# A stored instruction order in place of a list scheduler: four transformer layers on one Trainium2 core

## The chip, the cores and the metric

The kernel runs on one core of one Trainium2 chip. Five engines work side by side, each with its own queue that it takes in order: TensorE (PE: matmuls, and PEld for its weight loads), VectorE (DVE), ScalarE (ACT), GpSimd (POOL) and SyncE (SP), which here issues every DMA. The metric is device microseconds of one launch; the times shown are medians, and the profile is that of one execution.

## The reference

The input `x` has 2048 rows of 256 numbers (2 batches of 1024). It passes through four layers, each of a cross-attention and a feed-forward part, which makes eight sub-layers. The context has 77 rows per batch.

```python
x = x + tanh(g_xattn[0]) * attn(layernorm(x), ctx)                      # s0: one head of 256
x = x + tanh(g_ffn[0])   * fp4_ffn(layernorm(x), w_gate, w_up, w_down)  # s1: 704 wide, blocks of 16 rounded to fp4
x = x + tanh(g_xattn[1]) * mha(layernorm(x), ctx, Wq, Wk, Wv, We)       # s2: 16 heads of 16
x = x + tanh(g_ffn[1])   * (relu(layernorm(x) @ W1 + b1) @ W2 + b2)     # s3: 1024 wide
x = x + tanh(g_xattn[2]) * gated_mha(layernorm(x), ctx, w_q, w_kv, ...) # s4: 16 heads of 64
x = x + tanh(g_ffn[2])   * (layernorm(x) @ int4(kernel) + bias + lora)  # s5
x = x + tanh(g_xattn[3]) * mha(layernorm(x), ctx, Wq, Wk, Wv, Wo)       # s6: 16 heads of 16
x = x + tanh(g_ffn[3])   * moe(layernorm(x), 16 experts top 8 + shared) # s7
```

## The kernel before

**Tiles and tasks.** The rows are cut into eight chunks of 256 (`NU` chunks of `NT` = 2 tiles of 128 rows). A chunk going through one sub-layer is a task `u{chunk}s{sublayer}`, so `u5s4` is chunk 5 in sub-layer 4; 64 of these, plus tasks that prepare weights (`f0`, `h1`, `h1b0`, `a2`, `moe` and others). The chunks depend on each other nowhere; within a chunk, the sub-layers follow each other. `x` and all prepared weights stay on chip.

**Precision.** Nearly every product is made as three fp16 matmuls (`mm3`: high by high, high by low, low by high). Splitting a tile into its high and low half (`split`: one ACT pass and one DVE or POOL pass) and transposing it stand between one matmul and the next. Transposes go through PE (`pe_T`, with `ident`) or through a DMA transpose on SP's queue (`dma_T`: 132 of them, 64 on the `b` buffers, which carry probabilities and hidden rows, and 68 on the `m` buffers).

**Two passes of the builder.** `Builder` runs `program` twice. In the first pass no instruction is made: `Plan.note` records each call as an `Op`, with its engine, a duration and a latency by the formulas of `cost` and `dma_cost` (constants `XT`, `LAND`), the buffers that it uses, and the earlier calls that it must follow. Then `Plan.solve` decides the order. In the second pass `Builder.finish` (L558 to L564) issues the calls in `plan.order`, and each engine keeps that order. Every instruction is issued at L562, so the profile shows L562 throughout, and groups are told apart by their tiles. There are 11,317 calls: 6,875 for PE, 1,781 for DVE, 1,428 for ACT, 805 for POOL, 428 for SP.

**What sets the order.** `solve` (L228) is a list scheduler. It gives each call a key (the length of the chain of calls behind it, with a term `bias` for its chunk), runs `forward` (L292), an event-driven walk in which each idle engine takes the ready call with the least key, makes new keys with `backward` from the result, does so `ROUNDS` times, and keeps the best. At the end it adds `SHIFT`, a table of offsets, two per task, to the keys, and runs `forward` once more. `hold_back` (L207) adds edges that keep weight preparation from running too far ahead (`AHEAD`, `GATE`).

**Buffers.** Working tiles come from pools (`BUFFERS`, L48): 23 `m`, 4 `h`, 7 `b`, 32 `s`, 14 `q`, 8 PSUM banks `ps`, and five regions `R1` to `R5`. `forward` gives a tile its place when its first call starts in the walk, and frees the place when its last call ends there; `allowed` refuses a place that could lead to a deadlock. On the chip, the first call on a reused place waits for the last call on the tile that had it before.

Of the kernel before, what the change touches and what calls it, by code (L numbers as in the profile page):

```python
# [18 lines left out]
AX = mybir.AxisListType  # L19
# [3 lines left out]
P = 128  # L23
D = 256
S = 77
NU = 8
# [89 lines left out]
class Plan:  # L116
# [4 lines left out]
    def __init__(self):  # L121
        self.nc = bacc.Bacc("TRN2", target_bir_lowering=False, num_devices=1)
        self.ops = []
        self.places = {}
        self.bufs = []
        self.seen = {}
        self.tasks = []
        self.roots = {}
        self.gates = {}


    def task(self, label, *needs):

        at = {t[1]: i for i, t in enumerate(self.tasks)}
        self.tasks.append((len(self.tasks), label, [at[n] for n in needs if n in at]))
        if label[0] == "u":
            self.gates[int(label[3]), int(label[1])] = len(self.ops)
# [32 lines left out]
    def note(self, engine, name, a, k):  # L170
# [28 lines left out]
        if all(self.ops[j].task == 0 for j in op.pred):  # L199
            self.hold_back(i, op)  # L200
# [6 lines left out]
    def hold_back(self, i, op):  # L207


        label = self.tasks[op.task][1]  # L210
        if label == "setup":
            return
        if label[0] == "u":
            if not op.pred:
                op.pred[i - 1] = 0.0
            return
        roots = self.roots.setdefault(op.task, [])
        ahead = AHEAD.get(label, 3)
        if len(roots) >= ahead:
            j = roots[-ahead]  # L220
            j = max(self.ops[j].succ, default=j)
            op.pred[j] = self.ops[j].t
        elif label in GATE:
            op.pred[self.gates[GATE[label]]] = 0.0
        roots.append(i)


    def solve(self):  # L228


        ops = self.ops
        rest = [0.0] * len(ops)
        for i in range(len(ops) - 1, -1, -1):
            rest[i] = max([ops[i].t + ops[i].lat] + [ops[j].pred[i] + rest[j] for j in ops[i].succ])
        key = [bias(self.tasks[op.task][1]) - r for op, r in zip(ops, rest)]
        best = None
        self.ends = []
        for _ in range(ROUNDS):
            plan = self.forward([(k, i) for i, k in enumerate(key)])
            self.ends.append(plan[0])  # L240
            if best is None or plan[0] < best[0]:
                best, best_key = plan, key
            key = self.backward(plan[2])
        if SHIFT:
            best = self.forward([(k + 100.0 * d, i) for i, (k, d) in enumerate(zip(best_key, self.shifts()))])
            self.ends.append(best[0])
        self.end, self.place, self.start = best
        self.order = sorted(range(len(ops)), key=lambda i: (self.start[i], i))

    def shifts(self):  # L250

        n = len(self.tasks)
        first, last = SHIFT[:n], SHIFT[-n:]
        total = [0] * n
        for op in self.ops:
            total[op.task] += 1
        seen = [0] * n
        for op in self.ops:
            t = op.task
            yield first[t] + (last[t] - first[t]) * (seen[t] / (total[t] - 1) if total[t] > 1 else 0.0)  # L260
            seen[t] += 1

    def backward(self, start):


        ops = self.ops
        begin = [0.0] * len(ops)
        at = [op.t + op.lat for op in ops]
        left = [len(op.succ) for op in ops]
        ready = {e: [] for e in ENGINES}  # L270
        idle = dict.fromkeys(ENGINES, 0.0)
        events = [(op.lat, i) for i, op in enumerate(ops) if not op.succ]
        heapq.heapify(events)
        while events:
            now = events[0][0]
            while events and events[0][0] <= now:
                i = heapq.heappop(events)[1]
                if i >= 0:
                    heapq.heappush(ready[ops[i].engine], (-start[i] - ops[i].t, i))
            for e in ENGINES:  # L280
                if ready[e] and idle[e] <= now:
                    i = heapq.heappop(ready[e])[1]
                    begin[i] = idle[e] = now + ops[i].t
                    heapq.heappush(events, (idle[e], -1))
                    for j, p in ops[i].pred.items():
                        left[j] -= 1
                        at[j] = max(at[j], begin[i] + p)
                        if not left[j]:
                            heapq.heappush(events, (max(now, at[j] - ops[j].t), j))
        return [-b for b in begin]  # L290

    def forward(self, key):  # L292
        ops = self.ops
        n = len(ops)
        left = [len(op.pred) for op in ops]
        at = [0.0] * n


        last = {}
        for i, op in enumerate(ops):  # L300
            for b in op.bufs:
                last[b] = i
        uses = [0] * len(self.bufs)
        todo = [0] * len(self.tasks)
        claim = [dict.fromkeys(BUFFERS, 0) for _ in self.tasks]
        live = {}
        shared = {c for c, (_, m) in BUFFERS.items() if m == 1}
        turn = {}
        for i, op in enumerate(ops):
            todo[op.task] += 1  # L310
            for b in sorted(op.bufs):
                uses[b] += 1
                c, task = self.bufs[b]
                turn.setdefault(c if c in shared else (c, task), {})[b] = None
                if c not in shared:
                    now = live.setdefault((task, c), set())
                    now.add(b)
                    claim[task][c] = max(claim[task][c], len(now))
            for b in sorted(op.bufs):
                c, task = self.bufs[b]  # L320
                if last[b] == i and c not in shared:
                    live[task, c].discard(b)
        turn = {c: deque(q) for c, q in turn.items()}
        most = {c: max(t[c] for t in claim) for c in BUFFERS}
        free = {c: deque(range(m)) for c, (_, m) in BUFFERS.items()}
        held = [dict.fromkeys(BUFFERS, 0) for _ in self.tasks]

        def allowed(b):
            c, task = self.bufs[b]
            if turn[c if c in shared else (c, task)][0] != b:  # L330
                return False
            if not free[c]:
                return False
            if c in shared or len(free[c]) > most[c]:
                return True
            have = {d: len(f) for d, f in free.items()}
            have[c] -= 1
            held[task][c] += 1
            ended = set()

            def ends(t):
                if t in ended or not todo[t]:
                    return True
                if not all(ends(u) for u in self.tasks[t][2]):
                    return False
                if any(claim[t][d] - held[t][d] > have[d] for d in claim[t]):
                    return False
                for d, h in held[t].items():
                    have[d] += h
                ended.add(t)  # L350
                return True

            open_ = {t for t in range(len(self.tasks)) if any(held[t].values())}
            while open_:
                now = {t for t in open_ if ends(t)}
                if not now:
                    break
                open_ -= now
            held[task][c] -= 1
            return not open_  # L360

        place = {}
        stuck = []
        ready = {e: [] for e in ENGINES}
        idle = {e: 0.0 for e in ENGINES}
        queue = [0.0] * 16
        held_till = 0.0

        tick, columns, warm = 0, 0.0, False
        start = [None] * n  # L370
        events = [(0.0, 0, i) for i in range(n) if not left[i]]
        heapq.heapify(events)
        now = 0.0
        end = 0.0
        done = 0
        while events:
            now = events[0][0]
            while events and events[0][0] <= now:
                _, kind, i = heapq.heappop(events)
                if kind == 0:  # L380
                    heapq.heappush(ready[ops[i].engine], key[i])
                elif kind == 1:
                    again = False
                    for b in sorted(ops[i].bufs):
                        uses[b] -= 1
# [1228 lines left out]
```

## Time and profile before

| | |
|---|---|
| median of 7 runs | 869.66 us (865.59 to 873.34) |
| profiled execution, its own time | 869.66 us |
| its span, first to last instruction | 867.8 us |
| PE busy | 788.1 us (91%) |
| DVE busy | 682.8 us (79%) |
| POOL busy | 586.8 us (68%) |
| ACT busy | 553.0 us (64%) |
| mean granted PE clock | 0.956 |

The table's busy times are times in which at least one instruction of the engine was under way. A busy PE is not a PE at full pace: where the granted clock is low, the same matmul stays busy longer. The profile also gives the span in 40 slices, waits by the engine that ended them, and the busy time of each engine in any stretch that one asks for.

### The profile page before, as it was taken

How to read it: one execution, taken by the hardware profiler on the slowest of the kernel's cores; microseconds unless marked ns; L12 is line 12 of the kernel's file. 1: busy time of each engine (PE TensorE's matmuls, PEld its weight loads, DVE VectorE, ACT ScalarE, POOL GpSimd, SP SyncE). 2: the span in 40 equal slices, each digit the busy share in tenths (PEclk: the TensorE clock that was granted, in tenths of full speed). 3: DMA queues.
4: the chain of work that ended last, by engine and by line, in shares of the span. 5: the costliest groups of instructions: out<-in, count | busy, mean ns of one | idle time of the engine just before them, and what ended most of it. 6: DMA issues, size and time to landing. Idle time of an engine off the chain costs nothing.

```text
span 867.8 us, 20178 instructions
## 1 busy us (share of the span) xinstructions
PE 788.1 (91%) x6995; PEld 612.5 (71%) x6995; DVE 682.8 (79%) x1797; ACT 553.0 (64%) x1718; POOL 586.8 (68%) x809
## 2 busy tenths in 40 slices
PE   3889688998789999788998889999999999999998
PEld 2665355554576777566876677788888888888887
DVE  5778999998978977777888877869699886566544
ACT  5789673578674688999749888555465443233331
POOL 4455699999868868778979678967376553243332
PEclk9689799977899999899999999999999999999999
DMA  8453555698896659797996869792949455132411
GB/s 265 132 118 98 138 164 117 129 197 201 162 169 127 116 98 201 153 182 129 193 238 149 166 123 179 138 196 77 217 99 205 102 119 153 37 78 65 129 38 37
DMA packets 288175, 122.19 MB, mean 141 GB/s; under 512 B 236731, under 2 KB 276553, under 8 KB 287817
## 3 DMA queue, kind: packets, MB, share of 16 engines
q1 hardware_dynamic: 288073, 120.90, 64.0%
q8 instruction: 55, 0.90, 0.4%
q14 instruction: 47, 0.39, 0.1%
HBM read 53.71 MB, written 12.10 MB: 76 GB/s over the span
## 4 chain that ended last, share of the span: by engine, by line
PE 37%; DMA 8%; DVE 4%; POOL 3%; ACT 3%; issue 1%; SPq 0%; ACTq 0%; POOLq 0%; DVEq 0%
PE w_ps L562 37%; DMA w_b<-w_b 5%; ACT w_m L562 2%; DVE w_m L562 2%; POOL w_m L562 2%; DMA w_m<-w_m 1%; ACT w_b L562 1%; POOL w_b L562 1%; DMA w_m<-cd 1%; DVE w_s L562 1%; DMA w_b<-qd 0%; DVE w_b L562 0%; DMA qd<-w_m 0%; DVE x L562 0%; DVE w_ps L562 0%
## 5 line engine op out<-in xcount | busy, mean ns | idle before, releaser
L562 PE MATMUL w_ps<-w_m,w_R 128*128 128x256 f16 x2208 | 304.5, 274 | 6.1 <-DVE w_m L562 2.5
L562 PE MATMUL w_ps<-w_R,w_m 128*128 128x256 f16 (+4 forms) x1584 | 295.7, 306 | 7.0 <-DMA w_m<-w_m 2.1
L562 POOL TENSOR_TENSOR w_m<-w_m,w_m 128x256 f16<-128x256 f32 (+1 forms) x200 | 173.0, 878 | 141.6 <-ACT w_m L562 130.8
L562 PEld LDWEIGHTS <-w_m 128*128 128x128 f16 (+2 forms) x1936 | 181.5, 100 | 85.2 <-issue 19.0
L562 PEld LDWEIGHTS <-w_R 128*128 128x128 f16 x2208 | 214.4, 98 | 35.1 <-issue 5.8
L562 PE MATMUL w_ps<-w_R,w_b 128*128 128x256 f16 (+5 forms) x2352 | 210.2, 235 | 28.0 <-DMA w_b<-w_b 9.9
L562 ACT ACTIVATE w_m<-w_m 128x512 f16<-128x512 f32 (+7 forms) x230 | 118.9, 536 | 149.8 <-DVE w_m L562 130.4
L562 PEld LDWEIGHTS <-w_b 128*128 128x128 f16 (+2 forms) x2352 | 161.0, 98 | 68.4 <-issue 29.0
L562 ACT ACTIVATE w_m<-w_ps,w_s 128x77 f32<-128x77 f32 x528 | 146.6, 384 | 23.2 <-DVE w_s L562 15.6
L562 ACT ACTIVATE w_m<-w_ps 128x512 f32<-128x512 f32 (+6 forms) x192 | 93.4, 498 | 63.0 <-PE w_ps L562 47.3
L562 DVE SCALAR_TENSOR_TENSOR w_m<-w_ps,w_m 128x512 f32<-128x512 f32 (+3 forms) x160 | 103.5, 656 | 34.4 <-PE w_ps L562 26.9
L562 POOL TENSOR_TENSOR w_b<-w_m,w_b 128x462 f16<-128x462 f32 (+1 forms) x112 | 106.3, 962 | 31.3 <-ACT w_b L562 26.1
L562 DVE SCALAR_TENSOR_TENSOR w_m<-w_m,w_m 128x512 f32<-128x512 f32 (+3 forms) x92 | 76.8, 839 | 20.1 <-DMA w_m<-cd 11.8
L562 ACT ACTIVATE w_b<-w_m 128x462 f16<-128x462 f32 (+1 forms) x144 | 78.3, 583 | 2.3 <-PE w_ps L562 1.5
L562 DVE TENSOR_REDUCE w_ps<-w_ps 128x6 f32<-128x462 f32 (+2 forms) x104 | 56.1, 560 | 17.6 <-PE w_ps L562 16.5
L562 ACT ACTIVATION_READ_ACCUMULATOR w_m<-w_ps,w_s 128x1 f32 x272 | 66.3, 259 | 0.0
L562 POOL TENSOR_TENSOR w_b<-w_m,w_q 128x704 f16<-128x704 f16 (+2 forms) x48 | 53.5, 1132 | 6.2 <-DVE w_m L562 3.6
L562 POOL TENSOR_TENSOR w_s<-w_s,mhalf 128x2 f32<-128x2 f32 (+1 forms) x73 | 55.2, 759 | 3.5 <-DVE w_s L562 0.8
L562 DVE SCALAR_TENSOR_TENSOR x<-w_ps,sg_None,x 128x512 f32<-128x512 f32 (+1 forms) x56 | 37.3, 666 | 21.9 <-PE w_ps L562 21.6
L562 DVE BATCH_NORM_STATS2 w_s<-x 128x6 f32<-128x256 f32 x128 | 49.8, 410 | 6.0 <-DMA x<-in_x_dram 5.6
L562 POOL TENSOR_TENSOR w_m<-w_m,w_s 128x462 f32<-128x462 f32 (+1 forms) x48 | 43.3, 908 | 14.3 <-DVE w_s L562 11.5
L562 POOL TENSOR_TENSOR w_R<-w_m,w_R 128x512 f16<-128x512 f32 (+1 forms) x46 | 47.8, 1047 | 1.6 <-ACT w_R L562 1.1
(139 smaller groups left out, 1015.8 us busy)
## 6 DMA issues: line engine op xcount, KB each, us to landing
w_m<-cd SPq DMA_DIRECT2D x64, 256.0 KB
w_b<-qd SPq DMA_DIRECT2D x32, 256.0 KB
w_m<-in_l_gu_dram SPq DMA_DIRECT2D x17, 256.0 KB
qd<-w_m SPq DMA_DIRECT2D x16, 256.0 KB
w_m<-in_l_w_dram SPq DMA_DIRECT2D x10, 256.0 KB
AD<-w_h SPq DMA_DIRECT2D x8, 308.0 KB
w_R<-AD SPq DMA_DIRECT2D x2, 1232.0 KB
BD<-w_b SPq DMA_DIRECT2D x8, 308.0 KB
```

The source lines that it names most:

```text
L562: r = f(*a, **k)
```

## The change

The list scheduler goes (`forward`, `backward`, `shifts`, `hold_back`, `bias` and their tables). In its place stands `ORDER`, a compressed list of all 11,317 call numbers, found beforehand by a local search over an in-order simulation of the engines. `solve` unpacks it and hands out the buffers along it: a tile gets a place at its first call in the list, and the place goes back to the end of its pool's queue at the tile's last call in the list. The recorded calls themselves, the engine of each and the sizes of the pools stay. Two constants of the DMA cost formula change as well.

```diff
     def note(self, engine, name, a, k):
...
-        if all(self.ops[j].task == 0 for j in op.pred):
-            self.hold_back(i, op)
...
     def solve(self):
-        ops = self.ops
-        rest = [0.0] * len(ops)
-        for i in range(len(ops) - 1, -1, -1):
-            rest[i] = max([ops[i].t + ops[i].lat] + [ops[j].pred[i] + rest[j] for j in ops[i].succ])
-        key = [bias(self.tasks[op.task][1]) - r for op, r in zip(ops, rest)]
...
-        if SHIFT:
-            best = self.forward([(k + 100.0 * d, i) for i, (k, d) in enumerate(zip(best_key, self.shifts()))])
-            self.ends.append(best[0])
-        self.end, self.place, self.start = best
-        self.order = sorted(range(len(ops)), key=lambda i: (self.start[i], i))
+        steps = np.frombuffer(zlib.decompress(base64.b85decode("".join(ORDER))), "<i2")
+        self.order = [int(i) for i in np.cumsum(steps.astype(np.int64))]
+        assert sorted(self.order) == list(range(len(self.ops)))
+        uses = [0] * len(self.bufs)
+        for op in self.ops:
+            for b in op.bufs:
+                uses[b] += 1
+        free = {c: deque(range(m)) for c, (_, m) in BUFFERS.items()}
+        self.place = {}
+        for i in self.order:
+            for b in sorted(self.ops[i].bufs):
+                c = self.bufs[b][0]
+                if b not in self.place:
+                    self.place[b] = free[c].popleft()
+            for b in sorted(self.ops[i].bufs):
+                uses[b] -= 1
+                if not uses[b]:
+                    free[self.bufs[b][0]].append(self.place[b])
...
-XT = 20.0
-LAND = {"T": 1400.0, "R": 1900.0, "W": 500.0}
+XT = 22.0
+LAND = {"T": 1600.0, "R": 2200.0, "W": 600.0}
...
-AHEAD = {"a2": 6, "moe": 6, "f0": 9, "h1": 6, "h3": 6, "f1": 6}
...
-ROUNDS = 6
-
-SHIFT = [
-    -1145, 40, -1870, -735, 359, 42, 673, 54, -910, 81, -384, -5505, -489, -282, 121, 400, 154, 296, -437, -12,
...
-]
-BIAS = [i * 12 for i in range(8)]
...
+ORDER = (
...
+)
```

## The prediction

> **What bounds the kernel now.** I read the page first: busy shares, then the 40 slices, then the waits of PE, and then a table of stretches that I cut by PE's own progress.
>
> ```profile
> PE 788.1 (91%) x6995; PEld 612.5 (71%) x6995; DVE 682.8 (79%) x1797; ACT 553.0 (64%) x1718; POOL 586.8 (68%) x809
> ...
> PE   3889688998789999788998889999999999999998
> ...
> DVE  5778999998978977777888877869699886566544
> ...
> PEclk9689799977899999899999999999999999999999
> ```
>
> PE is the engine to feed, but the slices show two regimes. Up to the eleventh slice (239 us) DVE stands at 7 to 9 while PE has gaps and its granted clock falls; after that PE is nearly full, and over the last fifth it never stops.
>
> ```profile
> PE w_ps L562 <- DVE w_m L562: 12.3, 13, 2.1
> PE w_ps L562 <- DMA ident<-in_c_ident_dram: 12.0, 1, 12.0
> PE w_ps L562 <- DMA w_b<-w_b: 9.9, 10, 2.3
> PE w_ps L562 <- ACT w_m L562: 8.9, 12, 1.7
> PE w_ps L562 <- ACT w_b L562: 6.8, 10, 1.2
> PE w_ps L562 <- DVE w_q L562: 6.6, 3, 6.2
> ```
>
> No single wait is worth a prediction: apart from the start (12.0 us) and one of 6.2 us, they are 1 to 2 us each, ended by every engine and by DMAs. This is what an order can change, and it has to be summed by stretch.
>
> How the stretches were cut: I paired the n-th record of each engine with the n-th call of that engine in the order. For each shape of matmul I took a low (20th percentile) start-to-start time as its full-pace price: 109 ns for the 4,384 of 256 columns, 25 ns for those of 51 and fewer, 194 ns for 462. That makes 717.4 us of PE work, and the cuts lie at each twentieth of it (35.9 us). The last five are one line.
>
> ```profile
> 0.00:75.50 75.50, 55.60 (x333) 39.48 (x333) 53.75 (x203) 56.94 (x155) 37.80 (x59) 0.84 0.59 159
> 75.50:134.90 59.40, 47.09 (x256) 27.58 (x255) 57.07 (x146) 43.42 (x103) 46.78 (x40) 0.89 0.54 145
> 134.90:183.50 48.60, 43.62 (x242) 25.13 (x240) 44.60 (x120) 28.56 (x75) 46.21 (x48) 0.89 0.62 132
> 183.50:239.00 55.50, 47.36 (x374) 29.41 (x373) 51.17 (x131) 40.87 (x125) 48.39 (x64) 0.85 0.87 186
> ...
> 357.60:406.60 49.00, 40.97 (x399) 30.43 (x398) 33.07 (x106) 47.50 (x213) 36.10 (x59) 0.93 0.78 148
> 406.60:446.80 40.20, 37.73 (x414) 30.55 (x413) 34.59 (x87) 24.83 (x65) 33.04 (x65) 1.00 1.08 218
> 446.80:490.10 43.30, 38.89 (x306) 28.46 (x305) 36.82 (x108) 36.09 (x152) 36.97 (x59) 0.96 0.86 185
> ...
> 569.10:607.30 38.20, 36.62 (x360) 32.36 (x359) 29.95 (x60) 19.05 (x40) 28.52 (x42) 1.00 0.58 130
> ...
> 683.00:867.80 184.80, 180.73 (x1731) 159.98 (x1727) 115.95 (x239) 62.61 (x125) 68.61 (x71) 1.00 0.30 82
> ```
>
> Columns: stretch, length, busy time of PE, PEld, DVE, ACT, POOL, then granted clock. Length minus 35.9 is what a stretch loses. The span of 867.8 is 717.4 of work, 79.7 of idle PE (867.8 - 788.1) and 70.7 by which busy PE is slower than its full pace. Stage A (the first four stretches) takes 239.0 for 143.6 of work: 95.4 lost, with DVE busy 206.6. Stage B (239 to 683) takes 444.0 for 394.9: 49.1 lost, 13.1 of it in the one stretch where ACT is busy 47.5 of 49.0. Stage C loses 5.4.
>
> **The change, part by part.** *The calls.* The same 11,317 calls run on the same engines, DMAs included, so nothing is added to the sum, and the 717.4 stays.
>
> *The constants `XT` and `LAND`.* They feed durations of recorded calls; `solve` no longer reads durations. They cost and gain exactly nothing by themselves.
>
> *The order.* Comparing the two lists of calls: every engine's queue is reshuffled in the small (1,810 of PE's 6,874 neighbouring pairs survive, 184 of DVE's 1,780), but the large plan stays: by PE's progress half of PE's calls move by less than 3 us, and each task ends within some 25 us of where it did, bar a few preparations. I priced each engine's calls with their durations from this trace and summed them by twentieth of PE work.
>
> Stage A: DVE work before the cut at 143.7 us of PE work is 207.9 us in the old list and 205.5 in the new. So DVE leads this stage in both, and the change must gain by keeping it busy. The rows show how far that goes: DVE is busy 96%, 92% and 92% of the second to fourth stretch, and 78% of the first, counted from 6.75 us, when the timeline shows its first tile of `x` landing. The first stretch at 92% would take 53.4/0.92 + 6.75 = 64.8, or 10.7 less; the other three, with 2.1 us less DVE work at their own 93.5%, 2.2 less. Good end: -12.9. Bad end: 0, and below it the first rival.
>
> Stage B: the four stretches from 531 to 683 lose 1.8, 2.3, 2.6 and 1.3, a mean of 2.0. The six others (the ACT one aside) lose 28.0 together, so at that level they lose 12.0: -16.0. The ACT stretch: its ACT work goes from 47.8 to 47.2, and the stretches beside it are no lighter, so -0.6 and no more. Good end: -16.6. Bad end: 0.
>
> Stage C: PE is never idle until the tail, and the tail (the last residual, 0.75 us, then the last output DMA) stands in both lists: 0. The start: SP sends the 1 MB of `x` ahead of `ident` in both lists, so PE again begins near 12 us: 0.
>
> Between the ends, for A and B together (0 and -29.5), I take two thirds: most rows are already near the better level in the old order (seven of the ten counted lose under 4.5 us or have DVE at about 92% or more), so the level can be had with this mix; yet those rows have a lighter load or a standing bound. -19.7, which gives a span of 848.1. The execution's time stands 1.9 above its span and is the median of the runs: 850.0.
>
> *What a shorter wait saves.* Stretches are costed with idle time and slow pace together. In the two windows of 160 to 200 and 200 to 240 us the clock is 0.83 and 0.82 though PE's longest wait there is 1.8 us, so short waits do cost pace here. "TensorE: Matmul & The Clock Gate" of the Trainium skill, in its part on the clock gate, speaks against counting that: the clock falls after an idle window of about 3.4 us, so waits of 1 to 2 us would cost idle time alone. By that rule the gain would be 19.7 x 79.7/150.4 = 10.4, and the time 859; the two windows decide for the larger.
>
> *The DMA transposes.* Were the new list more generous to them? The chain shows 6.7 to 6.9 us for one on `w_b`, 4.6 to 4.8 on `w_m`. PE work between issue and first use is below that for 45 of 64 `w_b` transposes in both lists, and for 36 of 68 `w_m` in the old and 49 in the new. So nothing is gained there. (A place in the stored list is a rank, no time, so this is rough.)
>
> *The buffers.* The median PE work between the last use of an `m` place and its next tenant falls from 7.5 to 3.4 us, but the tight tenth stays (1.1, 0.9). On `b` the tight tenth gets looser (0.4 to 1.6). PSUM gets tighter: banks taken again within 0.3 us of PE work rise from 58 to 92 of 623. Bounds: 0, if the reader is done by then, and the second price below; I take 0, since PE's waits for readers of `ps` are in the stretches already.
>
> **The rivals.** *Slower: PSUM banks.* PE's queue is in order, so a matmul that waits for a bank holds all matmuls behind it, with the splits and softmax parts fed by them. If each of the 34 added tight reuses costs a read of a bank (rows of this page: 560 ns for the max, 656 ns for the subtraction; 0.61), that is 20.7 us idle, and at 150.4/79.7 = 1.89 of loss per idle us 39: 848.1 + 39 + 1.9 = 889. It decides once more than half of the 34 cost a full read. For it: the counts, and 13 waits of PE on DVE `w_m`. Against: PE's waits for such readers were under 2.1 us in a list that had 58 of these. Chance 0.20.
>
> *No change.* The large plan is the same, DVE's lead in A differs by 2.4 us and ACT's clump by 0.6. If the waits only move to other places, 868. For it: the transposes' cover, which did not grow. Against: waits of many small kinds are what a reshuffle reaches. Chance 0.12.
>
> *Much faster.* If A reaches DVE's floor (6.75 + 205.5 = 212.3, so -26.7), B gains its 16.0 and the ACT stretch loses 2.0 instead of 13.1, it is -53.8: 816. For it: the 150.4 us are all order and clock. Against: 47.2 us of ACT work stay in that stretch. Chance 0.12 for anything under 830.
>
> **How the numbers follow.** The forecast, 830 to 865, has 0.56. Faster by over 0.5% (4.3 us; about what a measurement of this kernel can tell) is that and the last rival: 0.68. Same 0.12, slower 0.20. The range goes down to 826, half way into the deep case, and up to 884, where three quarters of the bank price would lie; some 0.17 lies outside.
>
> **What would show it.** Right: PE idle time near 68 us, where 79.7 was; DVE busy at 90% or more up to PE's fifth of work, reached near 228 us; the PE clock in the first 12 slices above 0.86, its mean over 0 to 240 us now; the ACT clump still there at 360 to 405 us; the last 180 us without a gap. Wrong: PE waits on DVE and ACT tiles grown in number (bank rival), or the same sum in new places (no change), or no stretch with ACT near full (deep case). The sum fails if idle time falls without the clock rising, or if the DVE-led stage shortens by more than 13 us.

## The result: 3.8% slower, and the profile after

The changed kernel takes 903.0 us (median of 19 runs, 896.2 to 907.1) where the kernel before took 870.0 (47 runs): 1.0376 of it, with an interval of 1.0356 to 1.0397. The forecast was 850, the range ended at 884. The profiled execution spans 902.1 us.

First the page of the changed kernel: busy times, and PE, DVE and the PE clock in 40 slices.

```profile
PE 801.5 (89%) x6995; PEld 612.7 (68%) x6995; DVE 679.0 (75%) x1797; ACT 557.4 (62%) x1718; POOL 574.4 (64%) x809
...
PE   3898689887678799969888999999999999999998
...
DVE  5787888979657787856688888766988877567545
...
PEclk9979699989798999999899999999999999999999
```

PE's idle time went up from 79.7 to 100.6 us (902.1 - 801.5), and the slow pace of busy PE from 70.7 to 84.1 (801.5 - 717.4 of work at full pace). DVE, ACT and POOL do nearly the same work and are each a smaller share of the span: no engine became the bound. The engines wait more for one another.

Next, stretches of the changed kernel, cut at the same twentieths of PE work as in the prediction (35.9 us of work each; columns: stretch, length, busy PE, PEld, DVE, ACT, POOL, granted clock).

```profile
0.00:75.70 75.70, 55.12 (x333) 37.61 (x334) 55.90 (x202) 54.81 (x147) 35.01 (x59) 0.91 0.60 166
75.70:141.50 65.80, 52.99 (x254) 29.49 (x254) 54.24 (x142) 45.01 (x104) 45.37 (x43) 0.84 0.42 103
141.50:191.10 49.60, 44.18 (x243) 23.66 (x242) 42.81 (x121) 28.24 (x68) 45.72 (x48) 0.95 0.66 151
191.10:253.10 62.00, 47.38 (x374) 28.99 (x373) 49.41 (x134) 44.25 (x140) 42.99 (x59) 0.87 0.82 176
253.10:303.30 50.20, 41.87 (x371) 30.03 (x370) 34.40 (x96) 25.39 (x85) 31.42 (x51) 0.90 0.60 114
...
432.70:482.30 49.60, 42.37 (x415) 32.94 (x413) 34.75 (x82) 24.13 (x61) 30.79 (x66) 0.90 0.77 149
482.30:522.70 40.40, 37.41 (x301) 27.46 (x300) 34.33 (x107) 34.86 (x155) 34.98 (x49) 1.00 0.73 167
...
716.80:902.10 185.30, 180.89 (x1770) 160.08 (x1769) 120.56 (x243) 64.11 (x129) 68.87 (x72) 0.99 0.31 81
```

Of the kernel before, the prediction shows the first four stretches and the ninth (406.60:446.80); the fifth was this:

```profile
239.00:279.00 40.00, 37.73 (x377) 27.30 (x376) 33.16 (x95) 25.18 (x88) 29.27 (x46) 1.00 0.85 153
```

The loss is not spread out. Four of the twenty stretches carry it: the second (59.4 to 65.8 us), the fourth (55.5 to 62.0), the fifth (40.0 to 50.2) and the ninth (40.2 to 49.6): 32.5 us together, where the span grew by 34.3. Some others got shorter, as 482 to 523 (43.3 to 40.4). In the fifth and the ninth nothing is near full: DVE is busy 34.4 of 50.2, ACT 25.4, POOL 31.4. Something there makes idle engines wait.

The waits of the changed kernel name it: who waited for what, us in total, times, longest.

```profile
ACT w_m L338 <- DMA w_m<-w_m: 17.0, 8, 3.3
POOL w_b L338 <- DMA w_b<-w_b: 14.4, 4, 6.1
ACT w_b L338 <- DMA w_b<-w_b: 9.3, 6, 2.9
DVE w_b L338 <- DMA w_b<-w_b: 5.8, 3, 3.7
```

The same view of the kernel before has only these waits of ACT, POOL and DVE on DMAs that read a working tile, beside one of 1.5 us:

```profile
ACT w_h L562 <- DMA AD<-w_h: 2.9, 3, 2.0
POOL w_b L562 <- DMA w_b<-w_b: 2.8, 2, 2.4
ACT w_m L562 <- DMA w_m<-w_m: 1.9, 3, 1.5
```

`w_b<-w_b` and `w_m<-w_m` are the DMA transposes. ACT, POOL and DVE never read what these bring; only PE does. So when ACT waits for such a DMA before it writes a `w_m` tile, it waits for a buffer place that the DMA still reads. Counting every wait of ACT, POOL and DVE on a DMA that reads a working tile, it is 9.1 us before and 67.9 after. Of the 67.9, 31.9 wait for DMAs that read `m` places and 33.6 for those that read `b`.

One of them, in the timeline of the changed kernel (start, length, engine, operation; in brackets the idle time before it and who ended it):

```profile
267.18 3.05 SPq L338 DMA_TRANSPOSE w_b<-w_b  x1
...
267.61 1.05 ACT L338 ACTIVATE w_b<-w_ps 128x512 f16<-128x512 f32 x2
...
268.60 0.53 PE L338 MATMUL w_ps<-w_R,w_b 128*128 128x256 f16 x8
...
272.26 1.89 DVE L338 SCALAR_TENSOR_TENSOR w_b<-w_ps,w_b 128x512 f16<-128x512 f32 x3 [3.72 <-DMA w_b<-w_b]
...
273.01 0.87 PE L338 MATMUL w_ps<-w_R,w_b 128*128 128x256 f16 x6 [3.88 <-DVE w_b L338]
```

At 267.18 SP sends the probabilities of `u3s2` through a transpose. In the stored list that is the last call on their tile, so its place goes back to the pool there. Chunk 0's hidden rows of sub-layer 3 get that place. ACT has their high half done at once, in another place; DVE must write the low half and waits until the transpose reports its end, at about 272.2, some 5 us after SP began to send it. Behind DVE, PE stands for 3.88 us. (When the source alone had been read, the trace does not tell.) Over the whole changed kernel, the waits of ACT, POOL and DVE behind `w_b<-w_b` ended 3.6 to 6.6 us after SP began the transpose, and those behind `w_m<-w_m` 3.0 to 5.2 us after it.

In the lists of calls the difference is plain. A call's rank is its position in the list; the table gives the number of places that are taken again within 60 calls (some 4.6 us at 11,317 calls in 870 us) of the DMA that was the last to use them:

| order, handout | m (101 DMA readers) | b (69 or 70) |
|---|---|---|
| list scheduler, its own (place free at the planned end) | 8 | 1 |
| stored order, by rank (the change) | 42 | 12 |

### The profile page after: what moved, and what is told of

The parts are those of the page before. It is cut to its first block, busy times and chain, and to the rows that moved or that the text cites. A ratio compares the mean times of both kernels' runs of the same rounds, so it can differ in the third digit from the quotient of the medians.

```text
span 902.1 us, 20180 instructions
## 1 busy us (share of the span) xinstructions
PE 801.5 (89%) x6995; PEld 612.7 (68%) x6995; DVE 679.0 (75%) x1797; ACT 557.4 (62%) x1718; POOL 574.4 (64%) x809
## 5 line engine op out<-in xcount | busy, mean ns | idle before, releaser
L338 PE MATMUL w_ps<-w_R,w_m 128*128 128x256 f16 (+4 forms) x1584 | 364.6, 307 | 20.3 <-DVE w_q L338 4.1
L338 PE MATMUL w_ps<-w_m,w_R 128*128 128x256 f16 x2208 | 360.3, 273 | 12.7 <-DVE w_m L338 4.1
L338 PE MATMUL w_ps<-w_R,w_b 128*128 128x256 f16 (+7 forms) x2352 | 285.0, 237 | 29.0 <-DMA w_b<-w_b 7.5
L338 POOL TENSOR_TENSOR w_m<-w_m,w_m 128x256 f16<-128x256 f32 (+1 forms) x200 | 169.6, 861 | 152.4 <-ACT w_m L338 141.0
L338 PEld LDWEIGHTS <-w_R 128*128 128x128 f16 x2208 | 210.8, 98 | 47.1 <-issue 6.6
L338 PEld LDWEIGHTS <-w_b 128*128 128x128 f16 (+3 forms) x2352 | 185.0, 99 | 79.2 <-issue 23.1
L338 ACT ACTIVATE w_m<-w_m 128x512 f16<-128x512 f32 (+5 forms) x230 | 118.2, 534 | 94.8 <-DVE w_m L338 88.3
L338 POOL TENSOR_TENSOR w_b<-w_m,w_q 128x640 f16<-128x640 f16 (+2 forms) x48 | 49.6, 1048 | 8.4 <-DMA BD<-w_b 4.1
L338 ACT ACTIVATE w_b<-w_ps 77x512 f16<-77x512 f32 (+1 forms) x64 | 37.3, 596 | 23.0 <-PE w_ps L338 19.9
L338 ACT CAST w_m<-w_m 128x512 f16<-128x512 f32 (+1 forms) x53 | 31.8, 601 | 31.6 <-DVE w_m L338 30.4
```

The lines of the kernel that those rows point to most:

```text
L338: r = f(*a, **k)
```

## The experiments

The theory H: the handout under a DMA in flight is the loss, whatever the order. The rival O: the order of the engines' queues, PSUM banks included, is the loss. The handout can be changed with every queue left as it is, so the two come apart cleanly. Each ratio is to the kernel before on the same chip.

**The stored order with an aged handout.** A place whose last user was a DMA counts as freed 90 calls later; the place freed earliest is taken first.

```diff
-        free = {c: deque(range(m)) for c, (_, m) in BUFFERS.items()}
+        free = {c: [(i - m, i) for i in range(m)] for c, (_, m) in BUFFERS.items()}
...
-                    self.place[b] = free[c].popleft()
+                    at = min(free[c])
+                    free[c].remove(at)
+                    self.place[b] = at[1]
...
-                    free[self.bufs[b][0]].append(self.place[b])
+                    free[self.bufs[b][0]].append((k + (90 if self.ops[i].engine == "sync" else 0), self.place[b]))
```

> The stored order, every queue unchanged; only the handout of buffer places differs: a place whose last use is a DMA counts as freed 90 calls later, so it is handed out after others. Places taken again within 60 calls of a DMA's read fall from 42 to 3 on m and from 12 to 1 on b (the list scheduler's own handout had 8 and 1). Theory H (the handout under a DMA in flight stalls the writing engine): the stretches at PE work 144 to 179 and 287 to 323 us (+10.2 and +9.4 us) return and the one before the first of them by half, so some 20 to 25 us of the 33 are regained, 878 to 883 us, and the waits of ACT, POOL and DVE on DMAs that read buffers fall from 67 us to near 10. Theory O (the order of the engines' queues itself): 900 us or more, whatever those waits do.

Measured: 863.4 us against 873.3, ratio 0.988 (0.985 to 0.992). The page's first row and, of the view of waits, the one line of ACT, POOL or DVE on a transpose over 0.2 us:

```profile
PE 785.3 (91%) x6995; PEld 605.7 (70%) x6995; DVE 679.4 (79%) x1797; ACT 558.9 (65%) x1718; POOL 580.6 (67%) x809
```

```profile
POOL w_b L340 <- DMA w_b<-w_b: 1.5, 1, 1.5
```

The 67.9 us of waits are 1.9, PE's idle time is 77.0 us (862.3 - 785.3). The fifth stretch takes 43.1 us, the ninth 41.0, the second 61.0, the fourth 58.2. All 631 PSUM tiles keep the bank that they had in the changed kernel. So the whole loss, and more than I had expected, hangs on the handout of the other places. O falls. Those that move are places of `m`, `b` and `h`, and 265 of 491 `s` tiles, since places freed by the same call are now taken in another order. No `s` place has a DMA as its last user, and none is taken again within 160 calls of its last use. Nor is early reuse as such the cost: places that another engine than SP used last are taken again within 60 calls more often here than in the changed kernel (461 against 407 times on `m`, 49 against 29 on `b`).

The two times, 903.0 and 863.4 us, come from different sets of runs. In these times the handout cost 39.6 us; by the two ratios, 1.0376 and 0.9884, it is 43 us on a kernel before of 870.

**The list scheduler's order with the change's handout.** Only the places move; the order of before stands.

```diff
         self.order = sorted(range(len(ops)), key=lambda i: (self.start[i], i))
+        uses = [0] * len(self.bufs)
...
+        free = {c: deque(range(m)) for c, (_, m) in BUFFERS.items()}
+        self.place = {}
+        for i in self.order:
...
```

> The list scheduler's order, every queue unchanged, with the new handout (a place goes to the end of its pool's queue at its last use in the list). Places taken again within 60 calls of a DMA's read rise from 8 to 18 on m and from 1 to 8 on b, against 42 and 12 in the stored order. Theory H: slower by about a third of the 25 us that it puts on the handout, 875 to 880 us. Theory O: 868 to 872 us.

Measured: 912.3 us, ratio 1.044 (1.040 to 1.048). Waits of this kernel:

```profile
POOL w_b L577 <- DMA w_b<-w_b: 11.7, 5, 3.4
ACT w_b L577 <- DMA w_b<-w_b: 11.7, 4, 4.5
POOL w_m L577 <- DMA kd<-w_m: 4.8, 1, 4.8
```

The direction is H's, the size is not: I had priced it by the count of close reuses (18 and 8, against 42 and 12), and it cost as much as in the stored order. The waits on DMAs that read tiles sum to 47.3 us here; they are nearer to the loss than the count is.

**The cost doubled.** The same with places that a DMA has just been told to read preferred (they count as freed 60 calls earlier).

```diff
...
+                    free[self.bufs[b][0]].append((k + (-60 if self.ops[i].engine == "sync" else 0), self.place[b]))
```

> The list scheduler's order, every queue unchanged, with a handout that prefers places that a DMA has just been told to read (they count as freed 60 calls earlier): 34 on m and 24 on b are taken again within 60 calls of the read, about what the stored order has on m and twice on b. Theory H: 890 to 910 us, with ACT, POOL and DVE waiting 60 us or more on DMAs that read buffers. Theory O: within 5 us of before, 865 to 875.

Measured: 970.9 us, ratio 1.110 (1.105 to 1.116), beyond H's range. Its waits:

```profile
POOL w_b L579 <- DMA w_b<-w_b: 47.0, 10, 9.6
ACT w_m L579 <- DMA w_m<-w_m: 43.9, 15, 8.0
ACT w_b L579 <- DMA w_b<-w_b: 18.1, 4, 8.0
```

With the smaller ones they sum to 156.0 us, and 97.5 us of time were lost (970.9 - 873.3). So a us of such a wait cost 0.66 us here ((970.9 - 873.3) over 156.0 - 9.1), about 0.6 in the stored order (39.6 over 66.0), and 1.0 with the plain handout on the old order (39.0 over 38.2). The last of these has other waits of the handout in it, as the fourth corner below shows.

**The two pools apart.** The aged handout on one pool at a time, first on `m` (below), then with `"b"` in the same place.

```diff
-... (90 if self.ops[i].engine == "sync" else 0) ...
+... (90 if self.ops[i].engine == "sync" and self.bufs[b][0] == "m" else 0) ...
```

> The stored order; of the aged handout (90 calls for a place that a DMA read last) only the part on the m pool. Reuse within 60 calls of a DMA's read: 3 on m, 12 on b as in the stored order's own handout. The two pools share the 39.6 us between the stored order (903.0) and the aged one (863.4). Of the 67.9 us that ACT, POOL and DVE waited on DMAs reading buffers, 31.9 were on m and 33.6 on b. If a us of such a wait costs the same on both, 883 us. Against it: m has more of the close reuses (39 of 50 that go), which would give 872.

> The same with only the part on the b pool: 42 close reuses stay on m, 1 is left on b. By the waits 883 us, by the count of reuses 895. If both halves alone give more than their share (863 to 875 each), the stalls on the two pools follow from each other.

Measured: 888.4 us (1.022, 1.016 to 1.027) with `m` alone, 887.2 (1.019, 1.013 to 1.024) with `b` alone. Of the waits with `m` aged, those on `b` remain:

```profile
POOL w_b L340 <- DMA w_b<-w_b: 15.7, 5, 6.1
ACT w_b L340 <- DMA w_b<-w_b: 8.2, 6, 2.8
```

and the other way round:

```profile
ACT w_m L340 <- DMA w_m<-w_m: 17.0, 8, 3.0
POOL w_m L340 <- DMA w_m<-w_m: 6.9, 3, 3.9
```

The split by waits (883 and 883) was near, the one by counts (872 and 895) was off. Each alone regains some 15 us of the 39.6, both together 10 more than the sum (13 by the ratios). The reading that fits is that a stall on one pool is in part covered by a stall on the other; no run shows that by itself.

**Handing out by planned end, PSUM too.** Freed times from the planned duration and latency of the last use, at 13.2 calls per us: for all engines, and then for all but DMAs, which keep the 90.

```diff
-... (90 if self.ops[i].engine == "sync" else 0) ...
+... 0.0132 * (self.ops[i].t + self.ops[i].lat) ...
```

> The stored order; a place counts as freed later by the planned duration and latency of its last use, at 13.2 calls per us, for every engine. By this 9 close reuses on m and 2 on b are left, and only 201 of the 631 PSUM tiles keep their bank. If the close reuses under DMAs are the cause, 863 to 872 us; if the handout of PSUM banks matters beside it, it lies outside this, to either side.

> As the aged handout (90 calls for a DMA), and places that another engine used last count as freed later by that use's planned duration and latency at 13.2 calls per us. 3 close reuses on m, 1 on b, PSUM banks handed out by planned end. If only DMA readers matter, 861 to 866 us as with the aged handout; if banks handed out by rank still cost, 850 to 858.

Measured: 866.3 us (0.994, 0.990 to 0.998) and 867.7 (0.996, 0.993 to 0.999). Both spread the DMA readers, and both regain the loss, the second 2 us above what I had given it. PSUM banks were handed out anew in both (201 of 631 tiles keep theirs), and it gained nothing.

**The fourth corner, and the best again.** The list scheduler's order with the aged handout (the edit of the first experiment, after the old `solve`), beside a repeat of the first experiment.

> The list scheduler's order with the aged handout (90 calls for a DMA), the fourth corner of order by handout: 5 close reuses on m and 0 on b, against 8 and 1 in its own handout and 18 and 8 with the plain rank handout (912 us). If the close reuses under DMAs are all that a handout does here, 866 to 874 us, and the two orders then differ by the order alone, some 8 us. If the end that the list scheduler planned for each tile is worth more than this rule, 880 or more.

> The stored order with the aged handout once more, in more rounds, beside the list scheduler's order with the same handout: 860 to 866 us, 0.985 to 0.993 of before.

Measured: 880.0 us (1.010, 1.006 to 1.013) and 862.5 (0.989, 0.985 to 0.993). Now order and handout stand in a table, as ratios to the kernel before:

| | own, by planned end | by rank | by rank, DMA readers aged |
|---|---|---|---|
| list scheduler's order | 1 | 1.044 | 1.010 |
| stored order | - | 1.038 | 0.988, 0.989 |

Down each column the stored order is better: 0.994 by rank, where the two intervals only just do not touch, and clearly better with readers aged, 0.979 (0.9886/1.0098), 17.5 us (880.0 to 862.5). Along each row the change's handout is the worst. The 1.010 lies at the edge of my second case: on the old order, the planned ends are worth 1% (8 us) over the aged rule. The aged kernel still waits 17.3 us on DMAs that read tiles, where the kernel before has 9.1; at 0.66 to 1.0 us for each us of wait, that would be 5 to 8 us. No run takes this 1% apart.

**The constants alone.** The list scheduler with the two new DMA constants; then without its table of offsets, with the old constants and with the new ones (two executions each).

```diff
-XT = 20.0
-LAND = {"T": 1400.0, "R": 1900.0, "W": 500.0}
+XT = 22.0
+LAND = {"T": 1600.0, "R": 2200.0, "W": 600.0}
```

```diff
-SHIFT = [
...
-]
+SHIFT = []
```

> The list scheduler with the two new DMA constants and nothing else; it plans with longer DMAs, and its order moves. Theory H and theory O say little of it; if the constants make better plans, 860 to 868 us, if its tables of offsets only fit the old constants, 870 to 885 us.

> The list scheduler with the old DMA constants and without its table of offsets, with its own handout. The run with the new constants took 920 us (+5.3%). If that loss came from the table, which only fits the plan it was made for, this run loses about as much, 905 to 935 us; if the longer DMA constants are themselves the worse plan, this one lies within 10 us of before.

> The list scheduler with the new DMA constants and without the table. By the first reading (the table was the loss) as the run without the table and with the old constants, within 15 us of it; by the second, slower than that one by 40 us or more.

Measured: 920.3 us (1.053, 1.048 to 1.058) with the constants; 999.4 (1.146) without the table, and 956.7 (1.097) without it and with the new constants. All three expectations missed. The table is worth some 127 us to the old plan, far more than I thought. Without it the longer DMA times make the better plan, by 43 us; with it they make the worse one, by 47. So the offsets fit the plan they were made for and did not carry over to the one other plan tried. None of this is in the changed kernel, whose `solve` reads no durations.

## Why the prediction was wrong

*The order itself: near in sum, in part by luck.* The sum gave it -19.7 us: two thirds of 12.9 in stage A (the first four stretches) and of 16.6 in stage B. With the same aged handout under both orders it is worth -17.5 us; with places handed out by rank only 0.6%. The rows of stages A and B, cut as above, for the list scheduler's order with the aged handout:

```profile
0.00:248.20 248.20, 198.41 (x1199) 124.63 (x1200) 208.11 (x597) 170.82 (x454) 177.41 (x208) 0.86 0.64 151
248.20:695.40 447.20, 414.51 (x4069) 330.88 (x4068) 359.33 (x964) 320.62 (x1141) 338.92 (x531) 0.98 0.80 156
```

and for the stored order with it:

```profile
0.00:241.80 241.80, 192.72 (x1199) 116.84 (x1200) 204.34 (x596) 173.35 (x458) 174.91 (x210) 0.92 0.65 157
241.80:677.20 435.40, 411.94 (x4030) 328.88 (x4028) 355.04 (x960) 321.39 (x1133) 336.81 (x529) 1.00 0.80 158
```

Stage A goes from 248.2 to 241.8 us (-6.4 where 8.6 were forecast), stage B from 447.2 to 435.4 (-11.8, where 11.1 were). In B this is as forecast, a smaller loss in most stretches; 9.2 us of it are idle time of PE. In A it is not. The sum wanted DVE kept busier, from 86% of the stage in the kernel before to about 92%; it is 84% in both kernels here (208.1 of 248.2, 204.3 of 241.8). Nearly all of the gain in A is PE's pace (busy 198.4 to 192.7, clock 0.86 to 0.92), and beside the kernel before, whose stage A took 239.0 us, nothing was gained there at all. The ACT stretch stayed, some 48 us with ACT busy 47, as the sum had it.

*The failing step: "The buffers".* There I gave bounds and then took 0 for all pools, with a reason that speaks of PSUM alone (PE's waits for readers of `ps`). For `m` and `b` I had looked at the PE work between the last use of a place and its next tenant, for all readers together. The tight tenth barely moved on `m` (1.1 to 0.9) and got looser on `b`, and I called that harmless. But the readers are not alike. A pass of DVE is over 0.2 to 1.2 us after its start (the means of its rows in stage A of the kernel before); a DMA transpose of a `w_b` tile kept its source from the next writer for some 5 us after SP began to send it (267.18 to about 272.2 above). Of 837 reuses on `m` only 101 have a DMA as their last reader, and in the tenth of all they did not show. Counted apart, the new list had 42 of them close where the old one had 8. The price was the 39.6 us between 903.0 and 863.4 (43 by the ratios). With it the sum would have been 869.7 - 19.7 + 39.6 = 890, and the kernel before had a handout by planned end, worth another 8 us on its order: 898, against 903 measured. Both added terms are measured afterwards, so this closes the sum and is no forecast.

*Where the code said so.* `forward` frees a place when a call has ended in its walk, with its latency, and a DMA's latency contains the landing. The new `solve` frees it at the rank of the call. I described both in the account of the kernel and the change, and priced neither by what a DMA's end adds.

*The rival that ended slower.* It gave 889 by PSUM banks taken again early. The time was near, the mechanism wrong: the aged handout leaves every bank and every early reuse of one as it was, and is the fastest of all. Handing out banks by planned end gained nothing. The range's upper end, 884, was meant as three quarters of this rival's price; that is 879 (850 + 0.75 x 39).

*The signs.* What I had named for the bank rival was no sign of it. PE's waits on DVE `w_m` rose from 13 to 20 in number, as the bank rival asked. With readers aged there are 14, but those on ACT `w_m` are 21, in a kernel that is faster than before. The number of PE's waits tells little; what ended the waits of ACT, POOL and DVE told it at once.

*The transposes.* "Nothing gained" stands for the time from issue to PE's first use. I asked only when their output is ready, and never when their input is free again.

*The constants.* "Exactly nothing" holds for the changed kernel: only `dma_cost` reads them, and its `solve` reads none of the durations that come out.

*Pace and idle time.* I counted 0.89 us of slow pace with each idle us. Between the two kernels with readers aged it is 8.4 us of pace (76.3 to 67.9) with 9.6 of idle time (86.6 to 77.0): 0.88. From the aged run to the changed kernel idle time grows by 23.6 us and slow pace by 16.2 (84.1 - 67.9): 0.69. From the kernel before to the doubled run it is 102.6 - 70.7 = 31.9 with 69.2 idle, 0.46. So the ratio is no constant. "TensorE: Matmul & The Clock Gate" of the Trainium skill, in its part on the clock gate, lets the clock fall after an idle window of about 3.4 us; by that, shorter waits would have cost no pace. The waits added here reach 3.9 us, so these runs do not test the rule below its limit. The windows of the kernel before with clocks of 0.82 and 0.83 and PE waits up to 1.8 us still stand against it.

## What to carry to other kernels

When a plan hands out buffers, the free time of a place is the end of its last reader, and for the DMA transposes of the changed kernel that was 3 to 7 us after the queue began to send them. Count reuses by the engine of the last reader, DMAs apart; the count finds the trouble, the waits come nearer to its price. An order and its buffer handout are two changes: hold one fixed to price the other; here a better order (-2% with readers aged) was hidden under a handout that cost 4.6 to 5%. And in a profile with no full engine, look for compute engines that wait on a DMA whose result they never read: that is a buffer still held.

## What the runs showed that I had not expected

A handout alone, with the same instructions in the same order on every engine, moves this kernel from 862 to 903 us in one order and from 873 to 971 in the other. Aging the places of one pool regains 15 or 16 us, of both 40, so taking one kind of stall away shows less than its share. The stored order with DMA readers aged, at 862.5 to 863.4 us, is faster than both kernels, by 1.1% than the kernel before. The rule knows nothing but which engine used the place last.
